# Two clearings instead of one ahead of each paced row transfer, and ScalarE's first activation placed at the start, in a macaron block of two expert layers around an attention layer

## The chip, the core and the metric

The kernel runs on one core of a Trainium2 chip. Its engines work side by side and wait for one another through semaphores: TensorE (PE in the profile, PEld for its weight loads), VectorE (DVE), ScalarE (ACT), GpSimd (POOL) and SyncE (SP), which here does nothing but issue transfers. SP, ACT and GpSimd each issue transfers (DMA) in the order of their own instructions. The metric is the time of one execution in microseconds (us), as the median of several runs.

## The reference

The input x has 8 rows of 512 tokens, 128 numbers each. Three sublayers follow one another, each on a layer norm of x and each added to x:

```python
x = x + 0.5 * ffn(layernorm(x), gate_w, gate_b, w1, b1, w2, b2)
x = x + attn(layernorm(x), gamma, w_q, w_kv, w_out)
x = x + 0.5 * ffn(layernorm(x), gate_w, gate_b, w1, b1, w2, b2)
```

ffn is a layer of 8 experts. For each token a softmax over x @ gate_w.T + gate_b gives a share to each expert; the two largest count. An expert computes relu(x @ w1[e] + b1[e]) @ w2[e] + b2[e] with 512 hidden units. attn is a linear attention with 8 heads of 16: queries and keys are replaced by their Taylor terms up to the second order (1, the 16 numbers, and their products), the sum over all keys times values is formed once for each row and head, and each query is multiplied with it and divided by its own sum of weights.

## The kernel before, in words

All numbers are fp32. x stays on the chip (x_all), as 8 rows of four tiles of 128 tokens.

**Experts.** The kernel sorts tokens by expert instead of computing all of them. A Route (L569) takes one or two rows: normed (L514) makes the layer norm (statistics on DVE, the normalization itself on ACT, L555), PE turns it and multiplies with the gate (L590), DVE adds the bias (lg_f, L599) and finds the two best experts and each token's place in the sorted order (rows, L651). Then GpSimd sends each tile of 128 tokens twice, once for each expert, into the sorted buffer xg in DRAM, by an indirect transfer (L657) that writes each token to its own place. A Tiles object then takes tiles of 256 or 128 sorted tokens: SP loads xt (L799) and the expert's weights (L813, L815), PE turns the tile (L824), multiplies with w1 (L840) and w2 (L855), and turns it back (L864). In the first sublayer SP stores the result into yt (L877), and fetch (L1111) collects each token's two results with indirect transfers by GpSimd (L1122), 8 for each row, into got; added (L1129) adds them to x on DVE (L1136). In the second sublayer GpSimd itself stores each result to its token's place (L882). Unfilled places are set by transfers of nil (L408 at the start, L788 later).

The first sublayer handles rows 0 and 1 as one set and rows 2 to 7 as another (SETS, L29). Tiles go in phases: phase 0 has set 0 (15 tiles), phase 1 begins with what rows 2 to 5 are sure to fill (9 tiles), phase 2 has the rest. The first tile of a phase waits for all row transfers that it needs. In the second sublayer all 8 rows are one set and phase 0 needs rows 0 to 3.

**Attention.** Each row has a preparation (prep, L949: projections, products of keys), a core (squares of the queries on ACT, L1019, sums over keys on PE, L1032, their product, L1061 and L1063) and a tail (division, output product, added to x).

**What sets the order.** Every engine gets its instructions in the order of the source. While the program is written, a planner (Clock, L111) keeps an estimated time for each engine: 0.4 us for any GpSimd instruction that is not a transfer, 1.27 us for an indirect transfer. Work is cut into streams, and deal (L238) writes a side stream's next step as soon as its estimated start is no later than PE's. That start is taken as the later of DVE's and ACT's estimated times less a lead: LEAD, or LEADA during attention. Steps that use GpSimd alone take its estimated time instead. The planner decides places only; on the chip only the queues and the semaphores count.

**Pacing.** Ahead of an indirect transfer of L657 or L1122, pace() (L396) writes zeros to rest_area, 128 x 192 numbers that nobody reads, if clock.paced is set. It is set in the first sublayer's tile stage and in attention, and not in the first routing of rows 0 and 1 nor in the second sublayer's tile stage. So 144 of the 192 transfers of these two lines are paced.

**Start.** SP loads x, gamma and the attention weights. ACT issues four small loads (L271 to L275), then the three transfers of nil (L408), then its first computing instruction, the normalization of row 0. The tile which (33 x 1 numbers) gets its value later (L337).

Of the kernel before, what the change touches and what calls it, by code (L numbers as in the profile page):

```python
# [11 lines left out]
AF = mybir.ActivationFunctionType  # L12
# [9 lines left out]
E = 8  # L22
# [4 lines left out]
N = 256  # L27
# [17 lines left out]
SHIFTS = 7  # L45

PACED = (True,False)

AHEAD = 2
EARLY = 0.5  # L50
# [1 line left out]

SPARE = (2, 3)

LEAD, LEADA = 2.5, 3
FA = 128
FS = 160

# [2 lines left out]
def macaron_kernel(ctx: ExitStack, tc: tile.TileContext, x, gamma, w_q, w_kv, w_out, gate_wT, gate_b, w1, b1T, w2, b2, out):  # L61
# [9 lines left out]
    nc = tc.nc  # L71
# [6 lines left out]
    CAP = P << SHIFT  # L78
# [226 lines left out]
    last = const.tile([Q, 1], F32, name="last")  # L305
    spare = const.tile([Q, 1], F32, name="spare")
    which = const.tile([Q, 1], F32, name="which")
    b1T32 = const.tile([Q, P], F32, name="b1T32")
    nc.gpsimd.iota(iota_i, pattern=[[1, NTM]], base=0, channel_multiplier=0)
    nc.gpsimd.iota(qi[:, 0:1], pattern=[[0, 1]], base=0, channel_multiplier=1)  # L310
# [31 lines left out]
    def apart(i, keys, own):  # L342

        for key in keys:
            tc.declare_no_dep(i.ins, group=str(key), reason="rows of their own")
        for key in own:
            tc.add_to_no_dep_group(str(key), i.ins)
        alone.add(i.ins.name)
# [21 lines left out]
    nil = const.tile([P, N // P, WIDE], F32, name="nil")  # L370
# [12 lines left out]
    def rest_of(i, g, r):  # L383
        return xg[i][g][r].rearrange("(p u) d -> p u d", p=P)
# [9 lines left out]
    rest_area = const.tile([P, REST], F32, name="rest_area")  # L394

    def pace():  # L396

        if clock.paced:
            nc.gpsimd.memset(rest_area, 0.0)  # L399

    def sent(i, s, g, phase):

        apart(i, [("rows", s, g), *(("read", s, g, p) for p in range(phase))], [("rows", s, g), ("rows", s, g, phase)])
        written.setdefault((s, g, phase), []).append(i.ins.name)

    for i in range(2):
        for g in range(len(SETS[i])):
            sent(nc.scalar.dma_start(rest_of(i, g, slice(E * CAP, E * CAP + N)), nil), i, g, 0)  # L408

    order = const.tile([P, 1, E], F32, name="order")  # L410
    for e in range(E):
# [157 lines left out]
    class Route:  # L569
# [5 lines left out]
        def prep(self):  # L575
# [77 lines left out]
            for t in range(C):  # L653
                for k in range(2):
                    yield "pool"
                    pace()
                    i = nc.gpsimd.indirect_dma_start(  # L657
                        xg[s][g], bass.IndirectOffsetOnAxis(rows[s][:, k, b * T + t : b * T + t + 1], 0), xn[:, t, k], None
                    )
                    sent(i, s, g, phase)  # L660
# [227 lines left out]
    def tiles(ps, pool, steps, routing, sides):  # L888
# [5 lines left out]
        L = len(seq)  # L894
        clock.paced = PACED[steps[0].s]
        kept, keep = [], KEPT[steps[0].s]
# [214 lines left out]
    def fetch(group):  # L1111

        for u in group:
            b = u.b
            g = set_of[0][b][0]
            yield lambda: all_stored(0, g) and (b < GOT or units[b - GOT].fetched)
            u.got = work.tile([P, 2, T, D], F32, tag="got", name=f"got_{b}", bufs=GOT)
            yield "pool"
            for t in range(T):
                for k in range(2):  # L1120
                    pace()
                    i = nc.gpsimd.indirect_dma_start(  # L1122
                        u.got[:, k, t, :].bitcast(I32), None, yt[0][g].bitcast(I32), bass.IndirectOffsetOnAxis(rows[0][:, k, b * T + t : b * T + t + 1], 0)
                    )
                    behind(i, written["out", 0, g])
                    yield "pool"
            u.came = True
# [164 lines left out]
```

## Time and profile before

The median of 3 runs is 609.42 us (607.84 to 611.73). The profile is of another execution, with the profiler on.

| | us |
|---|---|
| profiled execution | 762.96 |
| its span, first to last instruction | 761.2 |
| PE busy | 566.1 |
| DVE busy | 314.1 |
| GpSimd busy | 307.2 |
| ACT busy | 265.3 |
| transfers of rows, L657, x128 | 132.2 |
| transfers of rows, L1122, x64 | 64.1 |
| clearings, L399, x144 | 39.5 |

The first sublayer lies from 0 to about 313 us, attention to about 531, the second sublayer from there. The mean granted clock of PE is 0.865 of full speed. A row of the timeline gives start, duration, engine, line, operation, what is written and read, the number of merged instructions, and in brackets how long the engine was idle before it and what released it. "issue" stands for time in which the profile shows nothing that was waited for.

### The profile page before, as it was taken

How to read it: one execution, taken by the hardware profiler on the slowest of the kernel's cores; microseconds unless marked ns; L12 is line 12 of the kernel's file. 1: busy time of each engine (PE TensorE's matmuls, PEld its weight loads, DVE VectorE, ACT ScalarE, POOL GpSimd, SP SyncE). 2: the span in 40 equal slices, each digit the busy share in tenths (PEclk: the TensorE clock that was granted, in tenths of full speed). 3: DMA queues.
4: the chain of work that ended last, by engine and by line, in shares of the span. 5: the costliest groups of instructions: out<-in, count | busy, mean ns of one | idle time of the engine just before them, and what ended most of it. 6: DMA issues, size and time to landing. Idle time of an engine off the chain costs nothing.

```text
span 761.2 us, 11281 instructions
## 1 busy us (share of the span) xinstructions
PE 566.1 (74%) x3239; PEld 407.3 (54%) x3239; DVE 314.1 (41%) x1185; ACT 265.3 (35%) x586; POOL 307.2 (40%) x452
## 2 busy tenths in 40 slices
PE   3248495379879999867878879988764956999950
PEld 2227474268757888422434424532653745888850
DVE  6625152123263565122944860760341431333325
ACT  3025321034224644414635553634211511444420
POOL 3522828800730000464780192192064364554440
PEclk9999857779989999978897995996785985999985
DMA  4135323357647655111110010010532543777728
GB/s 147 49 114 142 118 76 113 99 163 211 195 139 212 186 172 160 50 33 28 39 43 4 5 39 15 5 39 21 160 88 69 139 132 116 214 218 207 221 75 330
DMA packets 89392, 87.27 MB, mean 115 GB/s; under 512 B 10152, under 2 KB 70832, under 8 KB 89328
## 3 DMA queue, kind: packets, MB, share of 16 engines
q1 hardware_dynamic: 78464, 65.76, 30.1%
q0 software_dynamic: 8320, 17.19, 7.1%
q10 hardware_dynamic: 2544, 3.57, 1.3%
q8 instruction: 27, 0.44, 0.3%
q14 instruction: 37, 0.30, 0.1%
HBM read 62.57 MB, written 23.91 MB: 114 GB/s over the span
## 4 chain that ended last, share of the span: by engine, by line
PE 36%; issue 5%; another core or an unknown queue 5%; DVE 4%; ACT 4%; DMA 3%; POOL 1%; SPq 1%; DVEq 0%; ACTq 0%; POOLq 0%
PE ph_t L840 7%; PE py_t L855 6%; PE pz_a L1032 5%; PE pav_a L1061 3%; PE pav_a L1063 2%; PE pkv_a L962 2%; PE pf_a_rest L1015 2%; DMA fac<-yt 2%; PE pl_f L590 1%; DMA yt<-y_t,to_t 1%; ACT xn_f L555 1%; PE pt_t L824 1%; PE pq_a L970 1%; PE pd_a L1074 1%
## 5 line engine op out<-in xcount | busy, mean ns | idle before, releaser
L657 POOL DMA_INDIRECT xg<-xn_f,rows x128 | 132.2, 1033 | 188.2 <-issue 106.3
L840 PE MATMUL ph_t<-xT_t,w1t_t 128*128 128x256 f32 (+1 forms) x640 | 160.8, 400 | 3.2 <-DMA w1t_t<-in_w_dram 2.8
L855 PE MATMUL py_t<-h_t,w2t_t 128*128 128x256 f32 (+1 forms) x640 | 148.3, 375 | 2.8 <-issue 2.8
L840 PEld LDWEIGHTS ph_t<-xT_t,w1t_t 128*128 128x128 f32 x640 | 123.0, 213 | 20.5 <-DMA w1t_t<-in_w_dram 4.8
L1122 POOL DMA_INDIRECT got<-yt,rows x64 | 64.1, 1001 | 164.4 <-SPq L930 96.9
L855 PEld LDWEIGHTS py_t<-h_t,w2t_t 128*128 128x128 f32 x640 | 117.9, 197 | 19.2 <-issue 3.6
L847 DVE TENSOR_SCALAR h_t<-ph_t,bias_t 128x256 f32<-128x256 f32 (+1 forms) x160 | 66.7, 458 | 147.2 <-PE ph_t L840 84.5
L882 POOL DMA_INDIRECT yt<-y_t,to_t x68 | 65.1, 958 | 78.6 <-DVE to_t L829 56.3
L857 ACT ACTIVATE yT_t<-py_t,bias_t 128x256 f32<-128x256 f32 (+1 forms) x80 | 36.7, 458 | 167.5 <-PE py_t L855 119.6
L845 ACT ACTIVATE h_t<-ph_t,bias_t 128x256 f32<-128x256 f32 (+1 forms) x160 | 64.6, 455 | 73.0 <-PE ph_t L840 46.3
L824 PE MATMUL pt_t<-ident,xt_t 128*128 128x128 f32 x148 | 33.4, 306 | 48.8 <-DVE gone_t L775 16.7
L866 DVE TENSOR_TENSOR y_t<-py_t,xt_t 128x256 f32<-128x256 f32 (+1 forms) x80 | 32.2, 402 | 74.6 <-PE py_t L864 54.1
L1032 PE MATMUL pz_a<-fac,v 128*32 128x160 f32 x512 | 40.7, 324 | 21.5 <-issue 20.3
L824 PEld LDWEIGHTS pt_t<-ident,xt_t 128*128 128x128 f32 x148 | 20.1, 156 | 53.0 <-issue 20.7
L826 ACT COPY xT_t<-pt_t 128x256 f32<-128x256 f32 (+1 forms) x80 | 28.2, 354 | 50.4 <-PE pt_t L824 34.4
L1032 PEld LDWEIGHTS pz_a<-fac,v 128*32 128x32 f32 x512 | 19.2, 112 | 43.5 <-issue 40.1
L864 PE MATMUL py_t<-ident,yT_t 128*128 128x128 f32 x148 | 31.8, 292 | 13.3 <-issue 6.3
L399 POOL MEMSET rest_area<- 128x192 f32 x144 | 39.5, 275 | 0.1
L555 ACT ACTIVATE xn_f<-x_all,off_f,rs_w_f 128x256 f32<-128x256 f32 x64 | 32.4, 592 | 20.5 <-DVE bias_t L770 20.5
L1077 DVE TENSOR_SCALAR d_a<-pd_a 128x16 f32<-128x16 f32 x16 | 2.7, 171 | 74.4 <-PE pd_a L1074 70.2
L985 DVE TENSOR_TENSOR fac<-fac 128x896 f32<-128x896 f32 x32 | 33.1, 1081 | 0.0
L864 PEld LDWEIGHTS py_t<-ident,yT_t 128*128 128x128 f32 x148 | 20.6, 148 | 20.8 <-issue 7.4
(401 smaller groups left out, 705.8 us busy)
## 6 DMA issues: line engine op xcount, KB each, us to landing
w1t_t<-in_w_dram SPq DMA_DIRECT2D x80, 256.0 KB
w2t_t<-in_w_dram SPq DMA_DIRECT2D x80, 256.0 KB
xt_t<-xg SPq DMA_DIRECT2D x68, 130.0 KB
yt<-y_t SPq DMA_DIRECT2D x36, 128.0 KB
xg<-nil SPq DMA_DIRECT2D x24, 130.0 KB
x_all<-in_x_dram SPq DMA_DIRECT2D x8, 256.0 KB
xg<-xn_f,rows POOLq DMA_INDIRECT x128
fac<-yt SPq DMA_DIRECT2D x4, 512.0 KB
```

What stands on the lines that cost most here:

```text
L399: nc.gpsimd.memset(rest_area, 0.0)
L555: nc.scalar.activation(to, of, AF.Identity, bias=off[:, t : t + 1], scale=r[:, t : t + 1])
L657: i = nc.gpsimd.indirect_dma_start(xg[s][g], bass.IndirectOffsetOnAxis(rows[s][:, k, b * T + t : b * T + t + 1], 0), xn[:, t, k], None)
L824: nc.tensor.transpose(pt[:, bass.ts(u, P)], self.x[j][:, u, 0:D], ident)
L840: nc.tensor.matmul(ph[c // 2][:, c % 2, 0:n], lhsT=self.w[j][0][:, bass.ts(c, P)], rhs=self.xT[j], start=True, stop=True)
L845: nc.scalar.activation(h, ph[c // 2][:, c % 2, 0:n], AF.Relu, bias=bias)
L847: nc.vector.tensor_scalar(h, ph[c // 2][:, c % 2, 0:n], bias, 0.0, ALU.add, ALU.max)
L855: nc.tensor.matmul(py, lhsT=self.w[j][1][:, c, :], rhs=self.h[j][c], start=(c == 0), stop=(c == NC - 1))
L864: nc.tensor.transpose(pb[:, bass.ts(u, P)], self.yT[j][:, bass.ts(u, P)], ident)
L882: i = nc.gpsimd.indirect_dma_start(yt[self.s][self.g], bass.IndirectOffsetOnAxis(self.to[j][:, u : u + 1], 0), self.y[j][:, u, :], None)
L1032: nc.tensor.matmul(sums[slot, bass.ts(k, FS)], lhsT=self.v[:, t, 2 * j + k, :], rhs=self.fac[:, t, 2 * j + k, LIN : LIN + FS], start=(t == 0),
L1122: i = nc.gpsimd.indirect_dma_start(u.got[:, k, t, :].bitcast(I32), None, yt[0][g].bitcast(I32), bass.IndirectOffsetOnAxis(rows[0][:, k, b ...
```

## The change

Four edits:

- pace() clears rest_area twice instead of once.
- LEADA, the planner's lead in attention, goes from 3 to 2.
- ACT gets an activation (Identity) of the tile which as its first computing instruction, ahead of the transfers of nil; DVE zeroes which before.
- The three transfers of nil at the start (L408) are issued by SP and no longer by ACT.

```diff
 PACED = (True,False)
+RESTS = 2
...
-LEAD, LEADA = 2.5, 3
+LEAD, LEADA = 2.5, 2
...
     which = const.tile([Q, 1], F32, name="which")
+
+    nc.vector.memset(which, 0.0)
+    nc.scalar.activation(which, which, AF.Identity)
...
     def pace():
         if clock.paced:
-            nc.gpsimd.memset(rest_area, 0.0)
+            for _ in range(RESTS):
+                nc.gpsimd.memset(rest_area, 0.0)
...
-            sent(nc.scalar.dma_start(rest_of(i, g, slice(E * CAP, E * CAP + N)), nil), i, g, 0)
+            sent(nc.sync.dma_start(rest_of(i, g, slice(E * CAP, E * CAP + N)), nil), i, g, 0)
```

## The prediction

> **What bounds the kernel now.** I read the page's span and slices first, then busy time by stretch, then each engine in order of time at the places that the change touches, and last the waits of SP. No engine is full over the whole span (PE 74%, GpSimd 40%), so the sum has to be made stage by stage. The stretches are cut where GpSimd begins and ends a run of row transfers:
>
> ```profile
> 72.00:94.00 22.00, 12.71 (x63) 10.50 (x61) 6.87 (x31) 9.14 (x22) 19.24 (x32) 0.84 0.37 115
> ...
> 109.00:155.00 46.00, 22.26 (x97) 17.55 (x95) 10.71 (x54) 5.84 (x15) 39.60 (x64) 0.72 0.37 112
> 155.00:194.00 39.00, 36.59 (x189) 31.61 (x190) 12.87 (x35) 14.77 (x38) 0.00 (x0) 0.93 0.66 192
> 194.00:217.00 23.00, 17.33 (x76) 13.90 (x74) 5.22 (x18) 4.52 (x11) 19.62 (x32) 0.93 0.60 172
> 217.00:300.00 83.00, 78.94 (x407) 66.95 (x407) 49.52 (x153) 39.45 (x105) 0.00 (x0) 0.98 0.63 178
> ```
>
> The columns are length, then busy us of PE, weight load, DVE, ACT and POOL, then granted clock, DMA share and GB/s. Where GpSimd is silent, PE is busy 94 to 95% of the time (36.59 of 39, 78.94 of 83): PE is the bound there. Where GpSimd sends rows, PE is idle for 9.3, 23.7 and 5.7 us, although the DMA engines are at most 60% busy. The four runs in attention (313 to 352, 362 to 401, 435 to 462, 492 to 519 us) leave PE idle for 11.8, 7.3, 6.0 and 4.9 us. Together 68.7 us of PE idleness stand beside paced runs of transfers. The profiled execution takes 762.96 us and the median is 609.42, so 153.5 us exist only under the profiler. I take it that most of the 68.7 us is part of these 153.5; that is an inference from the size, not a reading.
>
> **The second clearing.** GpSimd's instructions in a paced run (start, us), and the page's group of the clearings (count, busy us, mean ns, idle before):
>
> ```profile
> 71.45 0.97 POOL L657 DMA_INDIRECT xg<-xn_f,rows  x1 [26.84 <-ACT xn_f L555]
> 72.42 0.27 POOL L399 MEMSET rest_area<- 128x192 f32 x1
> 72.85 0.96 POOL L657 DMA_INDIRECT xg<-xn_f,rows  x1 [0.16 <-issue]
> ```
>
> ```profile
> L399 POOL MEMSET rest_area<- 128x192 f32 x144 | 39.5, 275 | 0.1
> ```
>
> From start to start it is 72.85 - 71.45 = 1.40 us; transfers without a clearing start every 1.26 us (28.23 and 29.50). So the first clearing costs 0.14 us net, since most of it fits into a gap of 0.30 that is there anyway. A second one finds no gap left: it costs at most its own 0.27, and at least some 0.20, because clearings that follow one another overlap by about 0.06 (the two 256-column ones of fac take 0.58 together, a 260-column one alone 0.32). I take 0.24, so a period of 1.64. All 144 paced transfers get it: 48 of the first sublayer's routing, 64 of the fetch, 32 of the second sublayer's routing. That is 144 x 0.24 = 34.6 us more of GpSimd time. What of it reaches the end is decided by who waits for the last transfer of each run. From the transfer's end to its landing I allow 2.6 us (a row transfer of the second sublayer ends at 585.9 and the chain shows it landed at 588.5).
>
> First sublayer, sets of rows 2 to 7: the run from 71.45 (16 transfers) becomes 3.8 us longer and ends in the 15.57 us that GpSimd waits before 109.30. The run from 109.30 (32 transfers) becomes 7.7 us longer. The first reader is phase 1's first tile, the sixteenth load of xt, and it needs only the first half of that run:
>
> ```profile
> 153.75 0.27 POOL L399 MEMSET rest_area<- 128x192 f32 x1
> ...
> 168.76 0.35 SPq L799 DMA_DIRECT2D xt_t<-xg  x1
> ```
>
> That half is out at 131.3 and landed at 133.9, later at 137.7: 31 us of cover. Phase 2's first load (207.94) needs all 48: landed at 156.3, later at 164.0. If the cover were gone, all 32 transfers ahead of phase 1 would count, 7.7 us.
>
> Fetch of rows 0 and 1: out at 216.1, first added at 231.2; 3.8 us late leaves 8.7. Fetch of rows 2 to 7: row 2 is out at 324.0 and added at 339.21, where DVE stood behind a wait for PE; 8 x 0.24 = 1.9 us late is hidden. The later rows hang on a free buffer (GpSimd waits 5.55, 10.57 and 1.36 us for the adds), so they take the delay out of these waits. Behind a late add stands the whole DVE queue, so this would hurt if it were not hidden.
>
> Second sublayer's routing: the run from 435 grows into the 30.39 us wait before 491.92. The run from 491.92 ends at 518.45, landed 521.1, later 524.9. Its reader is the first xt load of the second sublayer; SP's longest wait before it, and the load itself:
>
> ```profile
> SPq L813 <- PE pav_a L1063: 26.2, 1, 26.2
> ```
>
> ```profile
> 534.65 0.87 SPq L799 DMA_DIRECT2D xt_t<-xg  x2
> ```
>
> SP stands behind a weight load that waits for attention's last product (531.02), so 9.7 us of cover remain. Gone, it costs 3.8 us. Sum for the clearing: 0, and 7.7 + 3.8 = 11.5 us with no cover.
>
> Here a rule speaks against the change. The Trainium skill, GPSIMD Engine Reference, section Key points: GpSimd shares its SBUF interfaces with VectorE and contends with instructions that have two SBUF inputs. Then 34.6 us more of clearing would slow such work. DVE's costliest of them, the product into fac, takes 1072 to 1087 ns in all 32 cases, beside transfers and clearings or not; what gives way is GpSimd, whose transfer takes 5.14 us at 440.69 beside four such products. If DVE lost the overlapped time (80 paced transfers lie in attention, where DVE is busy some 45% of the time: 80 x 0.24 x 0.45 = 8.6 us), attention could pay up to 9 us, an estimate; by the row it is 0. I take 0.
>
> **The early table and the three moved transfers.** Today ACT issues the three transfers of nil, and only then loads its table, at a moment when the first normalization is already waiting (its last operand, off, is ready at 8.76):
>
> ```profile
> 7.75 1.65 ACTq L408 DMA_DIRECT2D xg<-nil  x3
> 9.43 1.28 ACT L555 ACT_TABLE_LOAD   x1 [9.43 <-DMA x_all<-in_x_dram]
> 10.72 2.08 ACT L555 ACTIVATE xn_f<-x_all,off_f,rs_w_f 128x256 f32<-128x256 f32 x4
> ...
> 15.91 0.19 DVE L599 TENSOR_TENSOR lg_f<-pl_f,gb 128x32 f32<-128x32 f32 x1 [1.27 <-PE pl_f L590]
> ```
>
> After the change ACT's fourth transfer ends at 3.39, the table and a small Identity (0.2 us, as the ex_f row) are over before 5.1, and xn_f starts at 8.86: 1.86 us sooner. DVE's new clearing of which (about 0.15) lies in the first 3.57 us, in which DVE waits for x. The gain goes through PE and a copy to the lg_f row, where DVE had waited only 1.27 us; before that it is busy with statistics until 14.64. So 1.27 us is what passes; ACT's work on the second row starts 1.4 us sooner (at 12.4, when its off is ready, instead of 13.84), so that row doesn't cut the gain. From there DVE works without a gap to the first transfer of rows at 24.24, so all of the first sublayer moves by 1.27. The Trainium skill, ScalarE: Activation LUTs, section What ACT_TABLE_LOAD costs, has 1.28 us for the load plus 1.38 for a drain. The row shows the same 1.28, and the ACTIVATE begins 0.01 us after it: no drain. By the page ACT would gain 1.4 more; DVE's cap leaves 1.27 either way. Low bound 0, high bound 1.9.
>
> On SP the three transfers come after wo (issued until 8.30) and take 1.65 us, until about 9.95; SP's next work is at 31.27, so 21 us hide it.
>
> **LEADA, 3 to 2.** During attention the planner lets side work be written ahead of PE's plan by 2 us instead of 3, and counts two clearings as 0.8 us of GpSimd. Amounts stay the same, places shift by about 1 us, and the trace of before can't show the new order. In attention's chain the side work is xn_f 4.04 and fac 3.08 + 1.00, 8.1 us: the best is that all of it leaves the chain, the worst that as much joins it. I take 0, as near to either end.
>
> **Sum.** Profiled execution: -1.27 + 0 + 0 + 0; the median moves likewise, 609.42 - 1.27 = 608.1. In the profiled run alone PE's idleness may fall as well, by up to half of the 68.7 us.
>
> **Rivals.** (1) *Slower: GpSimd becomes the bound.* Without the profiler's stalls the tiles come sooner while GpSimd's pace stays. Between 58 and 168.7 us PE is busy 72.1 of 110.7; without stalls phase 1's load would come near 131, and the 32 transfers ahead of it, run on end from 71.45, land at 71.45 + 32 x 1.64 + 2.6 = 126.5. Five us decide. If both covers are gone: 608.1 + 11.5 = 619.6. For it: idle PE in just these stretches; against it: the covers above. (2) *Faster: slower sending relieves the others without a profiler too.* The stalls start 7.5 transfers into an unpaced run (24.24, first odd DVE gap at 33.6) and about 8.7 into a paced one (313.33, PE held from 325.4), so a slower pace puts them off; by these two points, to some 12 or 13 of 16 at 1.64, which halves them. If a quarter of the 68.7 us is there in plain runs, half of it is 9 us: 599. (3) *Slower through the new order:* 608.1 + 8.1 = 616. (4) *The change does nothing for the start* (ACT's gain eaten by DVE): 609.4, in the likeliest's range.
>
> **How the numbers follow.** Likeliest (608.1, own range 604 to 614): 0.52. GpSimd as bound: 0.22. Relief: 0.19. Order: 0.07. About 1% is what a measurement of this kernel can tell from no change: 603.3 to 615.5. So faster 0.19, same 0.52, slower 0.29. The range reaches to the centres of the two outer cases: 598 to 620.
>
> **What would show it.** Right: clearings x288, a paced period near 1.64, the table before 5.1, lg_f near 14.6, GpSimd's waits before 109 and 492 shorter, no wait of SP or PE for xg longer than now. Wrong: SP waiting at phase 1's first load or at the second sublayer's first load until a transfer of rows lands; side work of ACT or DVE on attention's chain beyond 8 us; a median moved by more than 6 us either way.

## The result, and the profile after

The changed kernel takes 632.14 us (629.65 to 633.08, 4 runs) against 608.63 us for the kernel before (607.26 to 611.73, 4 runs): ratio 1.036, 95% interval 1.032 to 1.040. The forecast was 608.1, with a range to 620. The change costs 23.5 us where a gain of one was expected.

The execution of 762.96 us whose lines stand in the prediction is of another kind than these runs: on some chips the kernel before takes some 750 us every time (part four of the experiments). So the lines of before below are from a second trace of it, on a chip where it takes 609 us. The page's head, first before, then after:

```profile
span 606.4 us, 11281 instructions
...
PE 505.4 (83%) x3239; PEld 377.4 (62%) x3239; DVE 314.5 (52%) x1185; ACT 264.2 (44%) x586; POOL 307.2 (51%) x452
```

```profile
span 627.9 us, 11428 instructions
...
PE 512.0 (82%) x3239; PEld 379.4 (60%) x3239; DVE 316.0 (50%) x1186; ACT 265.0 (42%) x587; POOL 342.5 (55%) x596
```

GpSimd is busy 35.3 us longer, DVE and ACT 1.5 and 0.8, and PE 6.6 (its mean granted clock is 0.943 instead of 0.952). That GpSimd's 35.3 lies near the 34.6 of the forecast is chance: busy time counts the clearings' own length, the forecast meant the delay of the transfers, and that came out larger, as shown below. Most of the 21.5 us is waiting. The same three stretches of both (first sublayer, attention, second sublayer; attention is cut from the first transfer of got for row 2 to the first weight load of the second sublayer; the last 2 to 3.4 us are left off), first before, then after. Columns: length, busy us of PE, weight load, DVE, ACT and POOL, granted clock, DMA share, GB/s.

```profile
0.00:252.70 252.70, 207.99 (x1129) 174.15 (x1129) 133.67 (x555) 99.15 (x247) 101.62 (x194) 0.98 0.61 175
252.70:413.20 160.50, 143.96 (x1284) 70.40 (x1285) 100.93 (x342) 99.83 (x179) 108.29 (x157) 0.96 0.12 34
413.20:603.00 189.80, 153.48 (x828) 132.83 (x826) 79.53 (x288) 65.21 (x162) 97.28 (x103) 0.92 0.66 196
```

```profile
0.00:259.10 259.10, 207.32 (x1129) 173.45 (x1129) 133.35 (x556) 99.77 (x248) 118.16 (x258) 0.97 0.59 170
259.10:441.60 182.50, 156.05 (x1312) 77.78 (x1313) 102.92 (x345) 101.76 (x183) 128.57 (x238) 0.93 0.11 30
441.60:626.00 184.40, 148.62 (x800) 128.21 (x799) 79.74 (x285) 63.47 (x158) 95.75 (x100) 0.92 0.67 203
```

6.4 us are lost in the first sublayer and 22.0 in attention; 6.8 come back in the second sublayer (190.5 to 183.7 us up to the last recorded instruction), of whose matmuls 28 now lie in attention. Attention is where the forecast had no wait to offer. GpSimd's paced run and the group of clearings, after:

```profile
65.94 0.96 POOL L662 DMA_INDIRECT xg<-xn_f,rows  x1 [21.95 <-ACT xn_f L560]
66.91 0.59 POOL L404 MEMSET rest_area<- 128x192 f32 x2
67.66 0.96 POOL L662 DMA_INDIRECT xg<-xn_f,rows  x1 [0.16 <-issue]
68.62 0.59 POOL L404 MEMSET rest_area<- 128x192 f32 x2
69.68 0.96 POOL L662 DMA_INDIRECT xg<-xn_f,rows  x1 [0.47 <-ACT yT_t L862]
```

```profile
L404 POOL MEMSET rest_area<- 128x192 f32 x288 | 76.7, 266 | 8.3
```

The period is not 1.64 us but 1.72 (31 of the second set's 47 steps) or 2.02 to 2.05 (15 of them), 1.81 in the mean: ahead of the slower ones GpSimd is idle for 0.47 us instead of 0.16. The start:

```profile
3.42 1.28 ACT L311 ACT_TABLE_LOAD   x1 [3.42 <-POOL nil L375]
4.72 0.20 ACT L311 ACTIVATE which<-which 33x1 f32<-33x1 f32 x1
8.79 2.08 ACT L560 ACTIVATE xn_f<-x_all,off_f,rs_w_f 128x256 f32<-128x256 f32 x4 [3.88 <-DVE off_f L549]
```

The table is over before 5.1, as forecast, and the first row's lg_f is at 13.99 (14.6 forecast, 15.75 before). But the first transfer of rows starts at 23.32 instead of 24.11, 0.79 us sooner and not 1.27: in the new order the second row's normalization comes later (15.32 instead of 13.68). Who waited for the sorted rows, in the views of waits of PE and of SP's queue (us in total, times, longest), first before, then after:

```profile
PE pt_t L824 <- DMA xt_t<-xg: 15.8, 6, 5.9
```

```profile
SPq L799 <- DMA xg<-xn_f,rows: 17.1, 11, 3.5
```

```profile
PE pt_t L829 <- DMA xt_t<-xg: 19.9, 4, 11.7
```

```profile
SPq L804 <- DMA xg<-xn_f,rows: 27.2, 12, 4.9
```

SP and PE wait some 4 to 10 us longer for row transfers. PE's longest, 11.7 us, is at phase 1's first tile (127.96), where it was 0.82 before, and ahead of it SP waits 4.9 us for rows to land. That is one of the signs that the prediction listed as proving it wrong. It belongs to the 6.4 us of the first sublayer; the 22 us of attention are something else.

### The profile page after: what moved, and what is told of

It reads as the page before. It is cut to its first block, busy times and chain, and to the rows that moved or that the text cites. A ratio compares the mean times of both kernels' runs of the same rounds, so it can differ in the third digit from the quotient of the medians.

```text
span 627.9 us, 11428 instructions
## 1 busy us (share of the span) xinstructions
PE 512.0 (82%) x3239; PEld 379.4 (60%) x3239; DVE 316.0 (50%) x1186; ACT 265.0 (42%) x587; POOL 342.5 (55%) x596
## 3 DMA queue, kind: packets, MB, share of 16 engines
q1 hardware_dynamic: 78896, 66.16, 36.9%
## 4 chain that ended last, share of the span: by engine, by line
PE 33%; DMA 6%; ACT 5%; DVE 4%; issue 4%; POOL 4%; SPq 2%; DVEq 0%; POOLq 0%; ACTq 0%
PE ph_t L845 7%; PE py_t L860 6%; PE pav_a L1066 3%; PE pav_a L1068 2%; PE pf_a_rest L1020 2%; PE pz_a L1037 2%; DMA fac<-yt 2%; POOL xg L662 2%; ACT xn_f L560 2%; PE pl_f L595 1%; DMA xg<-xn_f,rows 1%; PE pkv_a L967 1%; PE po_a L1107 1%; DMA xt_t<-xg 1%; POOL yt L887 1%
## 5 line engine op out<-in xcount | busy, mean ns | idle before, releaser
L845 PE MATMUL ph_t<-xT_t,w1t_t 128*128 128x256 f32 (+1 forms) x640 | 148.3, 376 | 5.5 <-DMA w1t_t<-in_w_dram 5.4
L860 PE MATMUL py_t<-h_t,w2t_t 128*128 128x256 f32 (+1 forms) x640 | 142.1, 365 | 0.6 <-DVE h_t L852 0.6
L845 PEld LDWEIGHTS ph_t<-xT_t,w1t_t 128*128 128x128 f32 x640 | 113.6, 197 | 20.2 <-DMA w1t_t<-in_w_dram 7.4
L860 PEld LDWEIGHTS py_t<-h_t,w2t_t 128*128 128x128 f32 x640 | 114.3, 191 | 14.7 <-DVE h_t L852 1.0
L404 POOL MEMSET rest_area<- 128x192 f32 x288 | 76.7, 266 | 8.3
L829 PE MATMUL pt_t<-ident,xt_t 128*128 128x128 f32 x148 | 31.2, 289 | 21.5 <-DMA xt_t<-xg 19.9
L990 DVE TENSOR_TENSOR fac<-fac 128x896 f32<-128x896 f32 x32 | 33.1, 1083 | 0.0
L569 PE MATMUL pt_f<-ident,xn_f 128*128 128x128 f32 x64 | 15.8, 347 | 18.8 <-ACT xn_f L560 14.7
L869 PE MATMUL py_t<-ident,yT_t 128*128 128x128 f32 x148 | 29.8, 276 | 1.1 <-ACT yT_t L862 0.6
L1037 PE MATMUL pz_a<-fac,v 128*32 128x160 f32 x512 | 21.4, 324 | 3.0 <-DVE fac L997 1.9
L569 PEld LDWEIGHTS pt_f<-ident,xn_f 128*128 128x128 f32 x64 | 9.0, 162 | 24.5 <-ACT xn_f L560 10.1
```

The lines of the kernel that those rows point to most:

```text
L829: nc.tensor.transpose(pt[:, bass.ts(u, P)], self.x[j][:, u, 0:D], ident)
L845: nc.tensor.matmul(ph[c // 2][:, c % 2, 0:n], lhsT=self.w[j][0][:, bass.ts(c, P)], rhs=self.xT[j], start=True, stop=True)
L860: nc.tensor.matmul(py, lhsT=self.w[j][1][:, c, :], rhs=self.h[j][c], start=(c == 0), stop=(c == NC - 1))
L869: nc.tensor.transpose(pb[:, bass.ts(u, P)], self.yT[j][:, bass.ts(u, P)], ident)
```

## The experiments

All ratios are against the kernel before on the same chip. Stages are read from each kernel's trace as above: start of attention, length of attention, and from there to the end.

**One: the parts alone.** The unchanged kernel, the second clearing alone (RESTS = 2), LEADA alone, and the start alone (the early activation, and the transfers of nil on SP).

> The kernel before, unchanged, for a second trace. If the stalls beside the row transfers in its first trace (68.7 us of TensorE idleness) belong to that one profiled execution, this trace's span is near 609 us and TensorE is busy over 85% beside the transfers. If they belong to every profiled execution of this kernel, the span is again above 700 us.

> Only the second clearing. Theory A (GpSimd becomes the bound: the second clearing costs more than the 0.24 us I took, and the tile loads wait for the row transfers to land): the whole loss, 628 to 634 us. Theory B (the new order in attention, from LEADA, is the loss): 607 to 612 us.

> Only LEADA 2 instead of 3. Theory A: 606 to 612 us, no change. Theory B: most of the loss, 622 to 632 us.

> Only the early activation and the three transfers of nil on SP. By both theories the prediction's 1.27 us sooner: 606.5 to 608.5 us. If it has a cost of its own (SP's queue), 610 us or more.

```diff
 second clearing alone:
-            nc.gpsimd.memset(rest_area, 0.0)
+            for _ in range(RESTS):
+                nc.gpsimd.memset(rest_area, 0.0)
 LEADA alone:
-LEAD, LEADA = 2.5, 3
+LEAD, LEADA = 2.5, 2
 start alone:
+    nc.vector.memset(which, 0.0)
+    nc.scalar.activation(which, which, AF.Identity)
-            sent(nc.scalar.dma_start(rest_of(i, g, slice(E * CAP, E * CAP + N)), nil), i, g, 0)
+            sent(nc.sync.dma_start(rest_of(i, g, slice(E * CAP, E * CAP + N)), nil), i, g, 0)
```

| kernel | median us | ratio (95%) | attention from | attention | after it |
|---|---|---|---|---|---|
| before, again | 608.83 | 0.998 (0.992 to 1.004) | 252.7 | 160.5 | 190.5 |
| second clearing | 629.47 | 1.030 (1.024 to 1.036) | 257.1 | 183.4 | 186.5 |
| LEADA = 2 | 621.70 | 1.018 (1.011 to 1.025) | 254.8 | 171.9 | 195.9 |
| start | 606.96 | 0.993 (0.987 to 0.998) | 249.3 | 160.9 | 191.0 |
| whole change | 632.14 | 1.036 (1.032 to 1.040) | 259.1 | 182.5 | 183.7 |

The second clearing brings the loss in attention by itself; LEADA brings a smaller one by itself; the two do not add up. The clearing does two things, though: it slows GpSimd on the chip, and the planner counts 0.4 us more for each paced transfer and so writes another order. The trace of LEADA = 2 is of the slowest of its four executions (627.01 us, median 621.70), so its stages are some 5 us long.

**Two: pace and order taken apart.** In the first kernel there are two clearings on the chip, and the planner counts 0.2 us for each, so that every engine's order is that of before. In the second there is one clearing, and the planner counts 0.8 us for it, so that the order is that of the second clearing alone.

> Two clearings on the chip, but the planner counts each at 0.2 us, so that the order of every engine's work is that of the kernel before; LEADA 3, old start. Theory G (GpSimd's slower pace makes others wait): 625 to 631 us, as with the second clearing alone. Theory P (the loss comes from the order, because the planner counts 0.4 us for the second clearing): 607 to 612 us, with the first sublayer some 0 to 4 us longer and attention near 160 us.

> One clearing on the chip, but the planner counts it at 0.8 us, so that the order is that of the run with the second clearing alone. Theory P: 625 to 631 us, attention above 178 us. Theory G: 607 to 611 us.

```diff
 pace alone (with the two clearings):
-                    cost = 0.4
+                    cost = 0.2 if any(a.bass_ap.tensor.name.startswith("rest_area") for a in outs) else 0.4
 order alone (with one clearing):
-                    cost = 0.4
+                    cost = 0.8 if any(a.bass_ap.tensor.name.startswith("rest_area") for a in outs) else 0.4
```

| kernel | median us | ratio (95%) | attention from | attention | after it |
|---|---|---|---|---|---|
| pace alone | 619.62 | 1.015 (1.011 to 1.018) | 256.5 | 160.9 | 195.7 |
| order alone | 626.47 | 1.024 (1.020 to 1.028) | 254.9 | 183.1 | 183.9 |

The order alone makes the whole loss in attention (160.5 to 183.1) without one more instruction on the chip. Pace alone falls between the two theories' ranges: it leaves attention as it was and still costs 9.0 us. How the order makes a row late is seen on DVE. In the kernel before, the add of got (L1136), with which a later row's preparation begins, stands ahead of the products into fac:

```profile
280.92 0.42 DVE L1079 TENSOR_TENSOR on_a<-pd_a,d_a 128x256 f32<-128x256 f32 x1
281.26 1.41 DVE L1136 TENSOR_TENSOR x_all<-x_all,got 128x512 f32<-128x512 f32 x2
...
288.29 0.68 DVE L1104 TENSOR_TENSOR x_all<-po_a,x_all 128x512 f32<-128x512 f32 x1
288.89 3.08 DVE L985 TENSOR_TENSOR fac<-fac 128x896 f32<-128x896 f32 x3
```

With the order alone changed:

```profile
283.17 0.42 DVE L1079 TENSOR_TENSOR on_a<-pd_a,d_a 128x256 f32<-128x256 f32 x1
288.61 0.69 DVE L1104 TENSOR_TENSOR x_all<-po_a,x_all 128x512 f32<-128x512 f32 x1 [5.01 <-PE po_a L1102]
289.21 0.67 DVE L978 TENSOR_REDUCE ksum_a<-fac 128x32 f32<-128x512 f32 x1
289.81 2.08 DVE L985 TENSOR_TENSOR fac<-fac 128x896 f32<-128x896 f32 x2
291.81 1.41 DVE L1136 TENSOR_TENSOR x_all<-x_all,got 128x512 f32<-128x512 f32 x2
```

The bracket of the add is empty in both: DVE does not wait for got, which has long landed. The add has been written behind an instruction that waits 5.01 us for PE and behind two products; DVE takes it in its turn at 36.9 us after attention's start instead of 28.6. On ACT this row's normalization (xn_a) has been written behind eight of the second sublayer's (xn_f), before and after:

```profile
291.77 1.64 ACT L555 ACTIVATE xn_a<-x_all,off_a,rs_w_a 128x128 f32<-128x128 f32 x4
```

```profile
307.46 4.04 ACT L555 ACTIVATE xn_f<-x_all,off_f,rs_w_f 128x256 f32<-128x256 f32 x8
311.40 1.63 ACT L555 ACTIVATE xn_a<-x_all,off_a,rs_w_a 128x128 f32<-128x128 f32 x4
```

It begins at 56.5 instead of 39.1 us after attention's start, and this row's projections on PE at 66 instead of 46. On the chain that ended last, xn_f holds 6.3% of attention with this order (11.5 us) and xn_a 3.3% (6.0 us); before, that chain does not reach back into attention. The planner's cause is its GpSimd time, as the one count is all that was changed: by its count the transfers of got end later, so it deals the work behind them later.

Pace alone costs 9.0 us of the median and 9.4 of the trace (606.4 to 615.8): 3.8 up to attention's start, 0.4 in attention, 5.2 after it. In its views of waits, PE first, then SP's queue:

```profile
PE pt_t L826 <- DMA xt_t<-xg: 24.2, 7, 10.9
```

```profile
SPq L801 <- DMA xg<-xn_f,rows: 27.4, 17, 3.8
```

PE's wait for a tile of sorted rows has grown from 15.8 to 24.2 us: at phase 1's tiles from 0.82 (at 120.26) to 4.85 (at 124.71), at the second sublayer's first tile from 5.46 to 10.89. These are the two places that the prediction's rival of GpSimd as the bound had named. The paced period is 1.87 us in the mean over the transfers of the second set, against 1.40.

**Three: is the old order special, and is the start worth anything?** LEADA at 4 together with the start; and the early activation alone.

> The early activation and the three transfers on SP, one clearing, and LEADA 4 instead of 3. If less lead makes the preparations late and the loss grows with each step down, a larger lead is no slower: 603 to 608 us. If every change of order away from the old one costs, as by chance: 612 us or more.

> Only the early activation; the three transfers stay on ACT, and no other instruction moves. By the prediction's sum the table leaves ACT's path, but ACT still issues the transfers until 9.40, so xn_f starts near 9.4 instead of 10.7: 1.27 us at most, 607.5 to 609 us. If the gain of the two edits together (some 2 to 5 us) is the changed order's and not the table's, this run shows 1.3 us or less of it.

```diff
-LEAD, LEADA = 2.5, 3
+LEAD, LEADA = 2.5, 4
```

LEADA = 4 with the start: 624.87 us, ratio 1.020 (1.016 to 1.024), attention 173.3, after it 197.9. So the planner's lead costs in both directions, though the amount of work is the same: 11 to 12 us in attention and 5 to 7 after it (this trace too is of the slowest execution, 626.63 us). In the kernel with LEADA = 2, what comes after attention is seen in SP's waits, whose longest for a landing of rows is now 16.2 us (3.5 before), because the run of transfers that it waits for begins 34.8 us after attention's end instead of 25.0:

```profile
SPq L799 <- DMA xg<-xn_f,rows: 26.4, 8, 16.2
```

The early activation alone: 608.73 us, ratio 0.998 (0.996 to 1.000), that is 1.3 us with an interval of 0.2 to 2.6; its first transfer of rows starts 0.96 us sooner. The start alone gains more, 0.7% (0.2 to 1.3%), or 2.5 us of the trace. There the order changes too, since ACT no longer issues nil; how much of the gain is the order's is not separated.

**Four: the same on chips where the kernel before takes 750 us.** The next four were meant for the same question (does the pace cost the same with the early start, is a truer count better, what does no clearing cost, what do two clearings in the first sublayer alone). They ran on a chip where the kernel before took 744.57 us (739.90 to 747.69) in all 11 executions. So they tell something else than what they were made for, and their expectations in us don't apply.

> The early activation and the transfers of nil on SP (606.96 us, ratio 0.9927, alone) together with a second clearing on the chip, while the planner counts 0.2 us for each clearing, so that every engine's order is that of the early start alone. If GpSimd's pace costs what it cost in the old order (+9.0 us of the trace, ratio 1.0147 alone), about 616, ratio 1.008. If the earlier start gives the tile loads more cover, or if pace costs only where the order is bad, 607, ratio 0.993. Between 610 and 613 would mean that the two parts share a wait.

> The early activation and the transfers of nil on SP, one clearing, and the planner counts it as the 0.14 us that the trace shows as its net cost instead of 0.4. If a truer count makes a better order, the mirror of the run in which counting 0.8 cost 2.4%: below 604, ratio 0.985 or less. If the places depend on the count as on a drawn lot, around the old order's neighbours: 615 to 625, as with LEADA at 2 and at 4. If only counts that delay GpSimd's side work hurt, 607, ratio 0.993, with attention's length at 161 us.

> No clearing on the chip at all; the planner still counts 0.4 us in its place, so every engine's order is that of the kernel before. With one clearing the time is 608.8, with two 619.6 in the same order. If only GpSimd's pace counts, none is faster: a step of 0.14 us instead of 0.38, so about 3 us less, 605, ratio 0.995, with PE's wait for xt from xg below 15.8 us. If slower sending relieves the transfers beside it (the forecast's rival of relief), none is slower than one: 613 or more, ratio above 1.006, with longer stalls of DVE or PE next to runs of transfers.

> The second clearing only in the first sublayer's tile stage (48 transfers of the routing and what of the fetch lies there), not in attention; the planner counts 0.2 each there, so every engine's order is that of the kernel before. If the two clearings cost at two separate places, +3.8 us of the trace here and 5.2 at the second sublayer's first load: about 612.5, ratio 1.006, the first sublayer's end 3.8 us later, the second sublayer's length as before (190.5). If the second sublayer's loss comes down from the first, the whole +9: 618, ratio 1.0147.

```diff
 start, with two clearings in its order:
+            for _ in range(RESTS):
+                nc.gpsimd.memset(rest_area, 0.0)
-                    cost = 0.4
+                    cost = 0.2 if any(a.bass_ap.tensor.name.startswith("rest_area") for a in outs) else 0.4
 start, one clearing counted as 0.14:
-                    cost = 0.4
+                    cost = 0.14 if any(a.bass_ap.tensor.name.startswith("rest_area") for a in outs) else 0.4
 no clearing:
-            nc.gpsimd.memset(rest_area, 0.0)
+            clock.look()
+            clock.free["Pool"] += 0.4
 two in the first sublayer only:
+            for _ in range(1 if clock.lead == LEADA else 2):
+                nc.gpsimd.memset(rest_area, 0.0)
-                    cost = 0.4
+                    cost = (0.4 if self.lead == LEADA else 0.2) if any(a.bass_ap.tensor.name.startswith("rest_area") for a in outs) else 0.4
```

| kernel | median us | ratio (95%) | attention from | attention | after it |
|---|---|---|---|---|---|
| start, two clearings | 667.86 | 0.898 (0.895 to 0.901) | 271.8 | 159.9 | 232.1 |
| start, counted 0.14 | 734.50 | 0.989 (0.985 to 0.994) | 302.4 | 191.7 | 232.5 |
| no clearing | 775.29 | 1.039 (1.033 to 1.045) | 328.8 | 216.7 | 227.1 |
| two in first sublayer | 702.79 | 0.946 (0.942 to 0.951) | 265.5 | 205.4 | 225.4 |

Here the clearing helps, and its help is local: with two of them in the first sublayer only, attention starts at 265.5 and still takes 205.4. The trace of 762.96 us (attention from 313.3, 217.7 long) is of this kind. So I ran the whole change and a series of doses (none, two and three clearings in the old order of every engine), again on one chip; it was another of this kind (before: 758.37 us, 752.50 to 761.62, 7 runs).

> The whole change once more, beside doses of clearing on one chip. On a chip where the kernel before takes about 609 us: 632, ratio 1.036, as measured. On a chip where it takes about 745 us with engines that stall beside runs of transfers: if the second clearing's relief holds whatever the order, near the 668 us of two clearings with the early start, plus the order's 20 us: 690, ratio 0.925. If the change only works in the old order: 740 or more.

> Two clearings on the chip in the old order of every engine. Plain chip: 619.6, ratio 1.0147, as measured. Stalling chip: relief theory 675, ratio 0.905 (the 668 us with the early start, less that start's gain); pace theory alone: slower than before by 9 us there too.

> No clearing on the chip in the old order of every engine. Plain chip: pace theory 605, ratio 0.995; relief theory 613 or more, ratio above 1.006. Stalling chip: ratio 1.039 as measured, 775 where before is 745.

> Three clearings on the chip in the old order of every engine (the planner counts a third of 0.4 us each). Plain chip: pace theory, a third clearing finds no gap and no cover, at least 0.27 us for each of the 48 transfers of the first routing's second set and 32 of the second sublayer: another 9 to 14 us over two clearings, 629 to 634, ratio 1.03 to 1.04. Stalling chip: relief theory, the stalls end altogether and the time nears that of a plain chip with three clearings, 640 or less, ratio 0.86; if two had already relieved all that can be, 675 plus the pace's 10 us.

```diff
 three clearings (two and none as above):
+RESTS = 3
-                    cost = 0.4
+                    cost = 0.4 / 3 if any(a.bass_ap.tensor.name.startswith("rest_area") for a in outs) else 0.4
```

| kernel | median us | ratio (95%) | period us | waits for "remote", us |
|---|---|---|---|---|
| no clearing | 775.15 | 1.023 (1.016 to 1.030) | 1.26 | 325.7 |
| one (before) | 758.37 | 1 | 1.40 | 164.6, in the trace of 762.96 |
| two | 664.98 | 0.876 (0.871 to 0.882) | 1.87 | 69.4 |
| three | 694.28 | 0.916 (0.909 to 0.923) | 2.18 | 72.4 |
| whole change | 681.22 | 0.899 (0.893 to 0.905) | 1.83 | 94.8 |

The last column sums the rows of the waits, over all engines, whose releaser is "remote" (another core or a queue that the profile doesn't know); engines that stand at the same time all count. Here "remote" means neither: of the 325.7 us with no clearing, 324.0 are waits for PE's own semaphore, whose increments the trace records 1.8 to 27 us after the recorded end of the matmul that makes them, too late for the view to pair the two. The traces of before, of pace alone and of the whole change at 609 to 632 us have no such row. With no clearing, GpSimd sends 16 transfers without a gap, up to 91.80, and DVE stands:

```profile
90.84 0.96 POOL L658 DMA_INDIRECT xg<-xn_f,rows  x1 [0.30 <-issue]
```

```profile
76.76 1.85 PE L591 MATMUL pl_f<-gwT,xnT_f 128*128 128x8 f32 x16
78.46 0.31 PE L865 MATMUL py_t<-ident,yT_t 128*128 128x128 f32 x1
94.97 0.47 PE L825 MATMUL pt_t<-ident,xt_t 128*128 128x128 f32 x1 [16.20 <-DVE lg_f L600]
```

```profile
DVE lg_f L600 <- remote: 18.8, 1, 18.8
```

DVE's next instruction reads pl_f, whose last matmul began by 78.6, and starts at 94.69, 2.9 us after the run of transfers is over; PE stands behind DVE, and ACT behind PE. Two clearings end nearly all of this where there are clearings. A third clearing takes no more of it away and costs 29 us over two: PE then waits 37.0 us for sorted rows instead of 21.4, and DVE 24.1 us for got instead of 7.1. That three would end the stalls is refuted. The whole change gains 10% on such a chip, and its order still costs there: 681.22 against 664.98.

**Five: the rest of the waits, and what they are for.** The waits left with two clearings lie beside the transfers of the second sublayer, which have no clearing. One kernel puts two clearings there too (not counted by the planner; on GpSimd some row transfers change places with stores of results, the other engines' orders stay). The other tests one idea of the cause, that DVE waits for the next block of its own instructions: no clearing, and 32 more instructions at DVE's start. Chip: before takes 747.21 us (744.14 to 752.61).

> Two clearings as in the old order, and two also ahead of the transfers of rows and of results in the second sublayer, which have none so far (100 transfers, period 1.26 to about 1.9 us). On a stalling chip: if speed of sending is what makes engines wait, the 69 us of remote waits left by two clearings nearly vanish and the time falls from 665 by some 20 to 30 us to about 640; if they have another cause, it rises by the pace. On a plain chip: pace alone, GpSimd sends without a gap for some 85 us of the second sublayer, so 10 to 30 us slower than two clearings: 630 to 650.

> No clearing, old order, and 32 more small instructions (clearing a tile of 33 x 1) at the start of DVE, while it waits for x. On a stalling chip: if DVE waits for the next block of its own instructions, its remote waits come 32 instructions earlier in its order at every one of the ten or so places (after 205, 276, 348, 520 and so on of the old instructions instead of 237, 308, 380, 552), ACT's stay where they were. If it waits for data or another queue, at the same operations as before. Time like no clearing, about 775. On a plain chip no remote waits, the time that of no clearing, within 3 us of 607.

```diff
 two in the second sublayer as well:
-        if clock.paced:
-            nc.gpsimd.memset(rest_area, 0.0)
+        if clock.paced or clock.late:
+            for _ in range(RESTS):
+                nc.gpsimd.memset(rest_area if clock.paced else rest_area[:, 1:REST], 0.0)
...
+                pace()
                 i = nc.gpsimd.indirect_dma_start(
 32 more on DVE (with no clearing):
+    for _ in range(32):
+        nc.vector.memset(which, 0.0)
```

Two clearings everywhere: 674.20 us, ratio 0.900 (0.895 to 0.906). The waits for "remote" fall to 3.5 us in one row, as the theory of the sending speed said; the gain that it promised does not come, since the same pace now makes GpSimd late in the second sublayer (242.6 us after attention's end against 232.8 with two clearings in part four, on another chip of that kind), and PE waits for the sorted rows instead:

```profile
PE pt_t L828 <- DMA xt_t<-xg: 56.6, 7, 25.1
```

32 more instructions: 772.71 us, ratio 1.033 (1.027 to 1.040). The wait of DVE does not move; it stands at the same operation:

```profile
74.35 0.22 DVE L552 SCALAR_TENSOR_TENSOR off_f<-twin_f,rs_w_f 128x8 f32<-128x8 f32 x1
93.23 0.22 DVE L607 TENSOR_TENSOR lg_f<-pl_f,gb 128x64 f32<-128x64 f32 x1 [18.66 <-remote]
```

That is the 270th recorded instruction of DVE instead of the 238th; the others stayed likewise (y_t at 414 instead of 382, d_a at 588 instead of 556). So DVE does not wait for blocks of its own instructions. What it waits for is PE's signal: with no clearing (part four), the two matmuls that start at 78.35 and 78.46 are recorded as ended by 78.77, but the increments of PE's semaphore come at 94.66 and 94.70; ahead of the stall that of a matmul ended at 73.37 came at 73.38. Nor do PE's instructions arrive late: from 71 to 100 us the view of the DMA queues lists no transfer of instructions for any engine. Whether the matmuls themselves or only their signals are held up stays open, as the profile models the ends of matmuls, and so does the reason.

## Why the prediction was wrong, point by point

- **"153.5 us exist only under the profiler": wrong.** Such times are there in every one of 25 executions of the kernel before on three chips and in none of 42 elsewhere (the timed runs and two more chips), and the second profiled execution took 608.13 us, the three beside it 607.94 to 613.08. So the sum was made on a trace of the other kind of chip, and the covers read from it (31 us at phase 1's load, 9.7 at the second sublayer's) are not there in the runs that were to be forecast: PE already waits there for rows, 0.82 and 5.46 us.
- **The failed step: LEADA and the planner's count, "I take 0, as near to either end".** The text names both (0.8 us instead of 0.4, places shifted by about 1 us) and bounds them by 8.1 us either way. The order alone, by the count, costs 18.1 us of the trace (606.4 to 624.5) and 15.9 of the median (ratio 1.024), LEADA alone 1.8% (ratio 1.018, some 11 us). The bound took as its measure the side work that could join attention's chain, and of each piece one run: 4.04 us for xn_f, of which three such runs lie in attention, so that xn_f alone holds 11.5 us of the chain. Beyond that, what moved was the beginning of whole rows' preparations, and with LEADA also the row transfers of the next stage. Rival 3 (616, chance 0.07) had the right kind, at less than half the size and the least chance. Zero was no middle either: on plain chips (those of 609 us) all three other orders that were forced by the count or the lead lost about 2%.
- **A second clearing's 0.24 us: mis-sized.** With pace alone it costs 1.87 - 1.40 = 0.47 us in the mean, in the whole change 0.41. The term came from the clearing's own length less an overlap of 0.06; two take 0.59 us, so the second adds 0.32, and the transfer after it starts another 0.3 us later every second or third time.
- **The clearings' delay, taken as hidden in the sum: wrong,** at the two places of rival 1. It gave 7.7 + 3.8 = 11.5 us with no cover; the pace alone cost 3.8 + 5.2 = 9.0. Its mechanism is shown by the order held fixed, and it explains under half of the loss.
- **The rule of the Trainium skill, GPSIMD Engine Reference, section Key points** (contention for SBUF), which by the prediction's estimate would have given up to 9 us in attention: taken as 0 by the row, and rightly. With pace alone attention is 160.9 us long instead of 160.5, and the products into fac take 1080 ns (1083 in the whole change) with two clearings, 1083 with one.
- **The start, -1.27: right in kind, not in its way to the end.** The table is at 3.42 with no drain behind it, the activation alone has the ratio 0.998, and SP's cover for the three transfers held. But 0.79 us of it reached the first transfer of rows (0.96 with the activation alone), since the order of the second row moved, which the text took as fixed.
- **Relief (rival 2, 599): not on the chips of the timed runs,** where no such wait is recorded and two clearings in the old order lose 1.5%. On the stalling chips it is what decides: the whole change there gives 0.899.

The parts add up only roughly: by the traces the order by the count 18.1, the pace 9.4, the start -2.5 (606.4 to 603.9) make 25.0 before LEADA, against 21.5. Order and pace overlap: the second clearing alone, which has both, costs 23.2 and not 27.5. LEADA changes another order than the one in which it was measured, so its own share in the whole is not known.

Left open: which order is good (the run with a truer count fell on a stalling chip, where 0.989 can't be split between order and relief); what no clearing costs or gains on a plain chip, for the same reason; and what differs between the chips. Each chip was met in one session, so even that it is the chip, and not its state at that hour, is not shown; and that a pause other than a clearing would relieve as much, no run shows. No version is best on both kinds: on plain chips the start alone (606.96, 0.993), on the others two clearings in the old order (664.98, 0.876).

## What to carry to other kernels

Where a program places its instructions by estimated costs, a change of an estimate is a change of the order of every engine, and is to be priced apart from the change on the chip: hold the order fixed by giving the new instructions the old count, and then change the count alone. If a profiled execution stands 25% above the timed ones, covers and waits are not to be read from it before it is known which of the two kinds the forecast is for. Slowing a sender can be a loss on one chip and a gain of 10% on the next, so such a constant is measured on several.

## What the runs showed of the hardware

- The same kernel takes 609 us on two chips and 745 to 758 us on three, each steadily (within 1% of its median). The slower ones show waits for PE's semaphore beside runs of indirect transfers, and their sum depends on the period: 326 us at 1.26 us (two more traces: 298 and 282), 165 at 1.40, 69 at 1.87, 72 at 2.18, where the pace's price has grown.
- A clearing of 128 x 192 between two indirect transfers takes 0.27 us and costs 0.14, a second one 0.47, a third 0.31: the starts come 1.72 and 2.02 us apart, mostly in turn, with two, 2.03 and 2.34 with three.
